# Layer 0 of a four-layer image network: the normalised attention output is loaded and projected by quarters of tokens, its weights by columns, and the bulk loads are placed step by step

## The chip, the cores and the metric

One core of one Trainium2 chip runs the whole program. The metric is the device time of one execution in microseconds (us), here the median of three executions. All arithmetic is fp32. One execution of the program was also recorded by the hardware profiler, and every reading of the profile below is of that execution.

## The reference, cut to what matters

The input `x` is 4 images of 512 channels by 32 x 32 = 1024 positions ("tokens"). Four layers follow one another, each normalising its input by groups of channels and adding its result to the input. Only layer 0 is changed here. It is an attention with 8 heads of 64 channels whose scores are mixed between heads, put through a softmax, and then normalised over each head's whole 1024 x 1024 map (mean, variance, `in_gamma`, `in_beta`):

```
attn = einsum('bhdq,bhdT->bhqT', q, k) * scale
attn = einsum('gh,bhqT->bgqT', w_head, attn)
attn = softmax(attn, axis=-1)
attn = (attn - mean) / sqrt(var + EPS) * in_gamma + in_beta
out  = einsum('bhqT,bhdT->bhqd', attn, v)
out  = out.reshape(b, t, c)
out  = out @ w_proj.T + b_proj
```

The `reshape` takes (head, query, channel of the head) straight to (token, channel). Head h therefore becomes tokens 128h to 128h + 127, and a pair of neighbouring heads becomes one quarter of the tokens. Because mean and variance are those of a whole head, the output `out` of an image can be scaled and projected only after its last query has been processed.

## The kernel before

**Stages.** Layer 0 takes the four images one after the other, until about 1270 us of the span. Then come one layer 2 attention per image and a last stage that looks up the 8 best rows of a memory for each token. The change touches the layer 0 stage alone.

**Steps.** `step` (line 1169) is called for steps s = 0 to 38 of each image; 32 of them (`STEPS`) start a block of 32 queries, the rest let the pipeline run empty. In a step of an image:

- `scores` (L449) multiplies q and k of block s on the TensorE (PE) into two PSUM pairs; the ScalarE (ACT) copies them to the tile `ss` (L455), and eight transfers of 128 KB, four issued by SyncE (SP) and four by GpSimd (POOL), regroup them by head into `s2` (L464). I call these eight the relay. Two tiles `ss` and two `s2` exist.
- `mix` (L475) of block s - 2 multiplies `s2` by the head weights; ACT takes the exponential (L482); the VectorE (DVE) transposes it (L488) and collects sums (L503).
- `apply` (L514) of block s - 7 multiplies the transposed exponentials by v.
- every fourth step `take_out` and `scale` bring the finished 128 queries to the tile `o` and SP stores them to the DRAM tensor `o_rows` (L593).

So the relay of block s must have landed for `mix` in step s + 2, and it must have left `ss` for the copy of step s + 2.

**Work of neighbouring images inside the steps.** While image b runs, the output of image b - 1 is finished: `collect` (L597) loads it back as `of`, in 8 pieces of 256 KB, and then `w_proj` as `w_p`, in 4 pieces of 256 KB; the generator `in_threes` issues three such loads a step, from step 7 on. `instance_norm` (L613) works out the factors in steps 3 to 6 and scales `of` on ACT (L639, 8 instructions) in steps 10, 11 and 12. Steps 12 to 27 (`OUT` = 12) each project one sixteenth: `put_quarter` (L687), four matmuls of 256 columns, then `add_to` and statistics on DVE; every second step ACT loads a piece `xr` of x and SP stores a finished piece to `x1`. At the same time `prepare` (L352) loads image b + 1 once by pieces `xs` for its statistics, and from step 28 (`NEXT`) `next_image` (L269) loads it again as `xn` (8 pieces of 256 KB) with `w_q` (4 pieces), again three loads a step. `normalized` scales `xn` on ACT in steps 30 and 31 and just after, and `take_q` projects it from step 32 on. For the last image the next one is image 0 of layer 2, and `put_out` (L695) projects the last output after the steps.

**Order and queues.** Nearly all instructions are pinned to program order. Bulk loads are issued from ACT's queue by `beside` (L258), and `early` (L1231) issues them between ACT's two `ss` copies of a step. `xn` and `of` share one SBUF place, the tag `xn`, taken in turn; `w_v`, `w_p` and `w_q` share the tag `w2`.

Of the kernel before, what the change touches and what calls it, by code (L numbers as in the profile page):

```python
# [16 lines left out]
P = 128  # L17
# [24 lines left out]
def fast_net(ctx: ExitStack, tc: tile.TileContext, a: dict, out: bass.AP, flag: bass.AP):  # L42
# [169 lines left out]
    dram = ctx.enter_context(tc.tile_pool(name="dram", bufs=1, space=bass.MemoryType.DRAM))  # L212
    x1 = [dram.tile([P, KC, T], F32, tag=f"x1_{b}", name=f"x1_{b}") for b in range(B)]
    x2 = [dram.tile([P, KC, T], F32, tag=f"x2_{b}", name=f"x2_{b}") for b in range(B)]
    o_rows = [dram.tile([P, TC, NB], F32, tag=f"o_{b}", name=f"o_{b}") for b in range(B)]
    r_rows = [dram.tile([NS, NS], F32, tag=f"r_{i}", name=f"r_{i}") for i in range(2)]


# [18 lines left out]
    o_full = eT_flat[:, 2 * KC * T:3 * KC * T]  # L237
    wp_full = eT_flat[:, 3 * KC * T:3 * KC * T + KC * C].rearrange("p (k c) -> p k c", k=KC)

    def big(tag, name):  # L240

        return apool.tile([P, KC, T], F32, tag=tag, name=name)
# [19 lines left out]
    def in_threes(loads):

        for i in range(0, len(loads), 3):
            for out, in_ in loads[i:i + 3]:
                beside(out, in_)
            yield

    def next_image(b, key, src):  # L269

        I = img[b]
        xn = I["xn"] = big("xn", f"xn_{key}{b}")
        w = I[key] = eight_k([P, KC, C], f"{key}_{b}", 2)
        return in_threes([
            (xn[:, k, n * NB:(n + 1) * NB], src[:, k, n * NB:(n + 1) * NB])
            for k in range(KC) for n in range(T // NB)
        ] + [(w[:, k], a[key][:, k]) for k in range(KC)])

    def run_out(gen):
        for _ in gen:  # L280
# [5 lines left out]
    def first():  # L286

        I = img[0]
        xn = I["xn"] = big("xn", "xn_0")
        w = I["w_q"] = eight_k([P, KC, C], "w_q0_0", 0)  # L290
        for k in range(KC):
            nc.sync.dma_start(out=xn[:, k, :], in_=x_v[0, :, k, :])
# [229 lines left out]
    def sums(b, j):  # L522
# [18 lines left out]
        pin(nc.vector.reciprocal(ri, ps))  # L541
        yield

        ok = small.tile([P, 2, NS], F32, tag="ok", name=f"ok_{nm}")
# [34 lines left out]
    def scale(b, j):  # L579


        I = img[b]
        rb = I.pop(("rb", j)).rearrange("p gp (q qq x) -> p qq gp x q", q=4, qq=2)
        pv = I["pv"].rearrange("p gp (qq x q) -> p qq gp x q", qq=2, q=4)
        o = apool.tile([P, KC, NH, NS // 2], F32, tag="o2", name=f"o_{b}_{j}")
        o_v = o.rearrange("p kc (gp r) x -> p r gp x kc", r=2)
        for r in range(2):
            h = slice(r * HD, (r + 1) * HD)
            for par in range(2):
                pin(nc.gpsimd.tensor_mul(  # L590
                    o_v[par * HD:(par + 1) * HD, r], pv[h, par], rb[h, par]))
            yield
        pin(nc.sync.dma_start(  # L593
            out=o_rows[b][:, j, :], in_=o.rearrange("p kc g x -> p (kc g x)")))
        yield

    def collect(b, last):  # L597


        I = img[b]  # L600
        if last:
            I["of"] = o_full
            nc.sync.dma_start(out=wp_full, in_=a["w_proj"])
            nc.sync.dma_start(out=I["of"].rearrange("p (j x) -> p j x", j=TC), in_=o_rows[b])
            return
        I["of"] = big("xn", f"of_{b}").rearrange("p k t -> p (k t)")
        of = I["of"].rearrange("p (j x) -> p j x", j=TC)
        yield from in_threes([(of[:, j], o_rows[b][:, j]) for j in range(6)])
        w = I["w_p"] = eight_k([P, KC, C], f"w_p_{b}", 2)
        yield from in_threes([(of[:, j], o_rows[b][:, j]) for j in range(6, TC)] + [  # L610
            (w[:, k], a["w_proj"][:, k]) for k in range(KC)])

    def instance_norm(b):  # L613


        I = img[b]
        red = small.tile([P, 1], F32, tag="red", name=f"red_{b}")
        pin(nc.vector.tensor_reduce(red, I["ssq"], AX.X, ALU.add))
        yield
        by_head = small.tile([P, NH], F32, tag="ssqh", name=f"ssqh_{b}")  # L620
        nc.gpsimd.tensor_scalar(by_head, of_head, red, None, ALU.mult)
        yield
        ps = small_ps(f"in_{b}")[:, 0:NH]
# [11 lines left out]
        nc.gpsimd.tensor_mul(bb, bb, I["vsum"])  # L635
        yield
        o = I["of"].rearrange("p (jk g x) -> p g jk x", g=NH, x=NS // 2)
        for g in range(NH):
            pin(nc.scalar.activation(  # L639
                o[:, g], o[:, g], AF.Identity, bias=bb[:, g:g + 1], scale=al[:, g:g + 1]))  # L640
            if g % 3 == 2:
                yield

    def out_view(b):
        return img[b]["of"].rearrange("p (j k g x) -> p k g j x", j=TC, g=NH, x=NS // 2)

    def image_piece(b, m, n):
        xr = img[b]["xr", m, n] = apool.tile(
# [11 lines left out]
    def piece_done(b, m, n):  # L660

        I = img[b]
        xr = I["xr", m, n]
        if n == 0:
            I["stb"] = small.tile([P, 2, 6], F32, tag="bnst", name=f"st_b{b}_{m}")
        if n == 0 and m == 0:
            I["mv"] = small.tile([P, KC, 2], F32, tag="mv", name=f"mv_b{b}")
        st, mv = I["stb"], I["mv"]
        pin(nc.vector.bn_stats(st[:, n, :], xr))
        if n == 0:  # L670
            return
        pin(nc.vector.bn_aggr(mv[:, m, :], st.rearrange("p i s -> p (i s)")))
        if m == KC - 1:
            mv1 = I["mv1"] = const.tile([P, 2, KC], F32, tag=f"mv1_{b}", name=f"mv1_{b}")
            pin(nc.vector.tensor_copy(mv1[:, 0, :], mv[:, :, 0]))
            pin(nc.vector.tensor_copy(mv1[:, 1, :], mv[:, :, 1]))

    def put_quarter(b, i):


        I = img[b]
        m, n4 = divmod(i, 4)
        Q = NB // 2
        ps = small_ps(f"p_{b}_{i}")[:, 0:Q]
        o = out_view(b)
        for k in range(KC):
            pin(nc.tensor.matmul(  # L687
                ps, I["w_p"][:, k, m * P:(m + 1) * P], o[:, k, 2 * n4:2 * n4 + 2],
                start=(k == 0), stop=(k == KC - 1),
            ))  # L690
        add_to(b, m, I["xr", m, n4 // 2][:, n4 % 2 * Q:(n4 % 2 + 1) * Q], ps)
        if n4 % 2:
            piece_done(b, m, n4 // 2)

    def put_out(b, m, at):  # L695
# [8 lines left out]
                piece_done(b, m, n)  # L704
                piece_out(b, m, n)

        project(wp_full, lambda k, n: o[:, k, 4 * n:4 * n + 4], m, at, add_out)

# [457 lines left out]
    for m in range(KC):  # L1166
        take_k(0, m, m + 1)

    def step(b, s, mid, piece):


# [6 lines left out]
        tiled = 0 <= j < TC  # L1178
        putting = b > 0 and OUT <= s < OUT + 16
        if b > 0 and OUT < s <= OUT + 16 and s % 2 == 0:  # L1180
            piece_out(b - 1, (s - 2 - OUT) // 4, (s - 2 - OUT) // 2 % 2)
        if s == 0:
            take_v(b, 0)
        if s < STEPS:
            scores(b, s, 0)
            early(b, s)
            scores(b, s, 1)
        if summing and at == 1:
            next(I["tail"])
        if putting:  # L1190
# [16 lines left out]
        if tiled and part == 3:  # L1207
            take_out(b, j)
        if b > 0 and OUT <= s + 1 < OUT + 16 and s % 2:
            image_piece(b - 1, (s + 1 - OUT) // 4, (s + 1 - OUT) // 2 % 2)  # L1210
        if not putting:
            mid(b, s)
        if tiled:
# [11 lines left out]

    OUT, NEXT = 12, 28
    state = {"behind": iter(()), "load": iter(())}

    def early(b, s):  # L1231

        if b > 0 and s == TC - 1:
            state["load"] = collect(b - 1, False)
        if s == NEXT:
            state["load"] = (
                next_image(0, "Wq", x1[0]) if b + 1 == B else next_image(b + 1, "w_q", x_v[b + 1]))
        next(state["load"], None)

    def mid(b, s):  # L1240
        before = b - 1
# [4 lines left out]
        if b > 0:  # L1246
            if s == 3:
                state["norm"] = instance_norm(before)
            if 3 <= s < 7 or OUT - 2 <= s <= OUT:
                next(state["norm"], None)  # L1250
            if s == NEXT:
                state["behind"] = chain(state["behind"], gating(before))
        if NEXT - 4 <= s:
# [11 lines left out]
    for b in range(B):  # L1265
        last = b + 1 == B
        nxt = img[0 if last else b + 1]
        keys = ("Wq", "Wk", "Wv") if last else ("w_q", "w_k", "w_v")
        state.update(held=False, ahead=prepare2(0, True) if last else prepare(b + 1))
        for s in range(STEPS):  # L1270
            step(b, s, mid, piece)
# [823 lines left out]
```

## Time and profile before

| | us |
|---|---|
| median of 3 executions | 2700.16 |
| the three | 2700.16, 2693.87, 2703.72 |
| the profiled execution, device time | 2703.81 |
| its span (first to last instruction) | 2702.0 |
| mean granted TensorE clock | 0.979 of full speed |

| engine | busy us | share of the span |
|---|---|---|
| PE (matmul) | 2581.5 | 96% |
| DVE | 1483.1 | 55% |
| POOL | 1236.2 | 46% |
| ACT | 996.4 | 37% |

The 16 DMA engines moved 349.81 MB, 129 GB/s over the span. Read the table with care: the shares are means over stages with different limits, and a matmul that is slow because the PE has just stood idle still counts as busy. What a stage loses shows in its own stretch of time.

### The profile page before, as it was taken

The numbers are of one execution on the slowest core, as the hardware profiler recorded it, in microseconds if no ns is written. First come the engines' busy times: TensorE is split into PE (matmuls) and PEld (weight loads), VectorE is DVE, ScalarE is ACT, GpSimd is POOL, SyncE is SP. The second block draws the span as 40 slices with busy tenths as digits, with TensorE's granted clock in tenths as the row PEclk, the third lists the DMA queues.
The fourth block names the chain that finished last, engine by engine and source line by source line (L and its number), as shares of the span: only waits on it lengthen the run. The fifth ranks groups of instructions, "written<-read, shape, count | busy, mean of one in ns | idle before, by whom it ended". The sixth has DMA issues, their size and how long they took to land.

```text
span 2702.0 us, 47106 instructions
## 1 busy us (share of the span) xinstructions
PE 2581.5 (96%) x18286; PEld 1156.0 (43%) x18286; DVE 1483.1 (55%) x2387; ACT 996.4 (37%) x1148; POOL 1236.2 (46%) x1891
## 2 busy tenths in 40 slices
PE   8998898989989899999999999999999999999995
PEld 3344433545345443545433443343344344444442
DVE  4487326862478507873145125324513437888886
ACT  1565335551465416651145035215403622121211
POOL 2266315662356524654067027205602626666664
PEclk9999999989999999999999999999999999999997
DMA  2477528881587617785310030021002016667665
GB/s 79 126 217 190 139 83 207 226 222 52 142 225 226 165 60 206 216 216 173 126 47 1 31 124 1 16 83 58 1 32 94 1 58 190 216 190 216 184 182 160
DMA packets 159320, 349.81 MB, mean 129 GB/s; under 512 B 32361, under 2 KB 65129, under 8 KB 155378
## 3 DMA queue, kind: packets, MB, share of 16 engines
q1 hardware_dynamic: 88608, 167.17, 20.4%
q0 software_dynamic: 49152, 142.79, 19.3%
q10 hardware_dynamic: 21330, 36.76, 5.0%
q8 instruction: 147, 2.41, 0.4%
q14 instruction: 83, 0.68, 0.1%
HBM read 178.57 MB, written 33.69 MB: 79 GB/s over the span
## 4 chain that ended last, share of the span: by engine, by line
PE 79%; DMA 5%; DVE 2%; ACT 1%; issue 1%; ACTq 0%; POOL 0%; SPq 0%; POOLq 0%
PE at L1101 16%; PE pair L193 9%; PE sc_c L980 9%; PE pv_c L1013 8%; PE pv L514 5%; PE pair L449 5%; PE p L193 4%; PE pair L475 4%; PE pt L408 3%; PE pt L687 3%; PE k L193 3%; PE q L193 3%; PE v L205 3%; DMA s<-ss 3%; PE rs_c L1034 1%
## 5 line engine op out<-in xcount | busy, mean ns | idle before, releaser
L488 DVE STREAM_TRANSPOSE eT<-e 128x1024 f32<-128x1024 f32 x256 | 315.1, 1231 | 280.8 <-ACT e L482 280.1
L464 POOL DMA_DIRECT2D s<-ss x512 | 259.4, 515 | 450.3 <-ACT ss L455 161.4
L1118 POOL DMA_INDIRECT got<-in_mem,ix x256 | 280.6, 1096 | 215.6 <-DVE tmx L1124 92.1
L503 DVE BATCH_NORM_STATS2 st<-e 128x6 f32<-128x256 f32 x1024 | 350.3, 403 | 1.9 <-POOL sqs L567 1.9
L974 ACT ACTIVATE eT<-sc_c 128x1024 f32<-128x1024 f32 x256 | 247.8, 1022 | 277.8 <-PE sc_c L980 216.4
L482 ACT ACTIVATE e<-pair 128x1024 f32<-128x1024 f32 x256 | 250.5, 1023 | 201.0 <-PE pair L475 179.6
L998 POOL TENSOR_TENSOR e<-eT 128x1024 f32<-128x1024 f32 x96 | 231.4, 2411 | 178.6 <-ACT eT L974 151.9
L455 ACT COPY ss<-pair 128x1024 f32<-128x1024 f32 x256 | 249.4, 1019 | 143.2 <-DMA s<-ss 64.9
L449 PE MATMUL pair<-k,q 64*32 64x512 f32 x4096 | 271.4, 618 | 18.7 <-ACT e L482 9.5
L999 DVE TENSOR_TENSOR eT<-eT,e 128x1024 f32<-128x1024 f32 x96 | 126.2, 1314 | 249.6 <-POOL e L998 249.5
L514 PE MATMUL pv<-eT,v 128*64 128x128 f32 x4096 | 256.9, 280 | 0.0
L514 PEld LDWEIGHTS pv<-eT,v 128*64 128x64 f32 x4096 | 226.6, 139 | 70.1 <-issue 68.5
L980 PE MATMUL sc_c<-q,k 64*128 64x512 f32 x1024 | 238.6, 605 | 2.3 <-DVE xr L653 2.3
L994 POOL TENSOR_TENSOR eT<-eT 128x1024 f32<-128x1024 f32 x32 | 80.6, 2518 | 346.8 <-ACT eT L974 333.6
L1013 PE MATMUL pv_c<-eT,v 128*64 128x512 f32 x1024 | 232.2, 596 | 0.0
L475 PE MATMUL pair<-s,wmix 32*32 32x512 f32 x4096 | 171.1, 630 | 37.1 <-DMA s<-ss 29.7
L1142 DVE SCALAR_TENSOR_TENSOR acc<-got,et,acc 128x512 f32<-128x512 f32 x224 | 168.5, 752 | 8.0
L1040 DVE RECIPROCAL ri_c<-ri_c 128x512 f32<-128x512 f32 x32 | 107.1, 3346 | 96.1 <-ACT ri_c L1039 96.1
L980 PEld LDWEIGHTS sc_c<-q,k 64*128 64x128 f32 x1024 | 94.1, 187 | 132.8 <-issue 73.6
L1106 ACT COPY att<-at 128x1024 f32<-128x1024 f32 x64 | 64.8, 1012 | 218.0 <-PE at L1101 217.8
L449 PEld LDWEIGHTS pair<-k,q 64*32 64x32 f32 x4096 | 59.2, 107 | 186.2 <-ACT e L482 75.3
L1013 PEld LDWEIGHTS pv_c<-eT,v 128*64 128x64 f32 x1024 | 70.4, 137 | 152.8 <-issue 152.2
(294 smaller groups left out, 3295.7 us busy)
## 6 DMA issues: line engine op xcount, KB each, us to landing
s<-ss SPq DMA_DIRECT2D x512, 128.0 KB
s<-ss POOLq DMA_DIRECT2D x512, 128.0 KB
rb<-r POOLq DMA_DIRECT2D x64, 128.0 KB
o<-o SPq DMA_DIRECT2D x32, 256.0 KB
xr<-in_x ACTq DMA_DIRECT2D x32, 256.0 KB
x<-xr SPq DMA_DIRECT2D x32, 256.0 KB
xr_c<-x SPq DMA_DIRECT2D x32, 256.0 KB
x<-xr_c SPq DMA_DIRECT2D x32, 256.0 KB
```

The source lines that it names most:

```text
L193: pin(nc.tensor.matmul(ps[:, n, :], w[:, k, m * P:(m + 1) * P], rhs(k, n), start=(k == 0), stop=(k == KC - 1),))
L449: pin(nc.tensor.matmul(sc[m * NS:(m + 1) * NS, r, :], q[r * HD:(r + 1) * HD, m, s * NS:(s + 1) * NS], k_[r * HD:(r + 1) * HD, m, n * NB:(n ...
L464: pin(relays[side].dma_start(out=s2[2 * m + r::NH], in_=ss[m * NS:(m + 1) * NS, r, :]))
L475: pin(nc.tensor.matmul(mixed(s, r // 2)[t * NS:(t + 1) * NS, r % 2, :].rearrange("p (qq k) -> p qq k", qq=2), wmix[r * NS:(r + 1) * NS], s ...
L482: pin(nc.scalar.activation(e[:, half].rearrange("p r qq k -> p (r qq k)"), flat2(mixed(s, half)), AF.Exp))
L488: pin(nc.vector.transpose(eT[:, j % 2].rearrange("p b (qq i r) x -> p i r qq b x", qq=2, i=4)[:, i, 2 * half:2 * half + 2], e[:, half].rea ...
L503: pin(nc.vector.bn_stats(st[:, i, 2 * half + r, qq, :], e[:, half, r, qq, :]))
L514: pin(nc.tensor.matmul(pv[r * HD:(r + 1) * HD, gp, :], I["v"][:, t, g * HD:(g + 1) * HD], eT[:, j % 2, t, :, 4 * g:4 * g + 4], start=(t == ...
L980: pin(nc.tensor.matmul(sc[:, r, :], I["k"][r * HD:(r + 1) * HD, m, t * P:(t + 1) * P], I["q"][r * HD:(r + 1) * HD, m, n * NB:(n + 1) * NB] ...
L1013: pin(nc.tensor.matmul(pv[r * HD:(r + 1) * HD, :], I["v"][:, t, h * HD:(h + 1) * HD], e[:, r, :], start=(t == 0), stop=(t == TC - 1),))
L1101: pin(nc.tensor.matmul(sc[:, n * NB:(n + 1) * NB], xn3[b][:, k, tt * P:(tt + 1) * P], memT[k][:, i0:i0 + NB], start=(k == 0), stop=(k == K ...
L1118: pin(nc.gpsimd.indirect_dma_start(out=got[:, i, :], out_offset=None, in_=a["mem"], in_offset=bass.IndirectOffsetOnAxis(ap=ix[:, i:i + 1], ...
```

## The change

The layout of `o_rows` becomes [partition, head pair, block of queries, 128] instead of [partition, block, 512], and the tile `o` follows it; each store still has 256 KB, now in runs of 512 bytes in DRAM. One tile `xn_all` is allocated once and serves as `xn` and as `of`, so that parts of it can be loaded and used on their own. The projection runs by quarters: units are ordered by token half first, then by output channels, so that steps 12 to 19 need quarters 0 and 1 of `of` and steps 20 to 27 quarters 2 and 3. The scaling moves to quarters as well (two ACT instructions each in steps 10, 11, 18 and 19). Weights `w_p` and `w_q` are loaded by 128 output columns, in runs of 512 bytes, instead of by 128 input rows, in runs of 2 KB. The three-a-step generator is replaced by a plan that names the loads of each step.

| loads of 256 KB, by step | 7 | 8 | 9 | 10 | 11 | 12 | 13 | 14 | 15 | 16 | 17 | 20, 22, 24, 26 | 28 | 29 | 30 | 31 | 32 | 33 |
|---|---|---|---|---|---|---|---|---|---|---|---|---|---|---|---|---|---|---|
| before | 3 | 3 | 3 | 3 | | | | | | | | | 3 | 3 | 3 | 3 | | |
| after | 2 | 1 | 1 | 1 | 1 | 1 | 1 | 1 | 1 | 1 | 1 | 1 each | 2 | 2 | 1 | 1 | 1 | 1 |

(Rows from 7 to 17 hold for images 1 to 3, the others for all four. Weight columns are the loads of steps 10, 11, 12, 14 and 30 to 33.) `put_out` of the last image now also multiplies by quarters: 64 matmuls of 256 columns where there were 32 of 512. Two small tiles change their number of buffers (`ok` 4 to 2, the statistics `st_b` to one tile of four).

```diff
-    o_rows = [dram.tile([P, TC, NB], F32, tag=f"o_{b}", name=f"o_{b}") for b in range(B)]
+    o_rows = [dram.tile([P, KC, TC, P], F32, tag=f"o_{b}", name=f"o_{b}") for b in range(B)]
+    xn_all = apool.tile([P, KC, T], F32, tag="xn", name="xn_all")
...
     def next_image(b, key, src):
-        I = img[b]
-        xn = I["xn"] = big("xn", f"xn_{key}{b}")
-        w = I[key] = eight_k([P, KC, C], f"{key}_{b}", 2)
-        return in_threes([
-            (xn[:, k, n * NB:(n + 1) * NB], src[:, k, n * NB:(n + 1) * NB])
-            for k in range(KC) for n in range(T // NB)
-        ] + [(w[:, k], a[key][:, k]) for k in range(KC)])
+        def half(k, n):
+            def load():
+                I = img[b]
+                I["xn"] = xn_all
+                beside(xn_all[:, k, n * NB:(n + 1) * NB], src[:, k, n * NB:(n + 1) * NB])
+            return load
+        halves = [half(k, n) for k in range(KC) for n in range(T // NB)]
+        plan = {NEXT - 8 + 2 * i: halves[i:i + 1] for i in range(4)}
+        plan |= {NEXT + i: halves[4 + 2 * i:6 + 2 * i] for i in range(2)}
+        plan |= {NEXT + 2 + m: [load_columns(b, key, a[key], m)] for m in range(KC)}
+        return plan
+    def load_columns(b, key, src, m):
+        def load():
+            I = img[b]
+            if m == 0:
+                I[key] = eight_k([P, KC, C], f"{key}_{b}", 2)
+            beside(I[key][:, :, m * P:(m + 1) * P], src[:, :, m * P:(m + 1) * P])
+        return load
...
-        o = apool.tile([P, KC, NH, NS // 2], F32, tag="o2", name=f"o_{b}_{j}")
-        o_v = o.rearrange("p kc (gp r) x -> p r gp x kc", r=2)
+        o = apool.tile([P, KC, KC, 2, NS // 2], F32, tag="o2", name=f"o_{b}_{j}")
+        o_v = o.rearrange("p gp kc r x -> p r gp x kc")
...
-            out=o_rows[b][:, j, :], in_=o.rearrange("p kc g x -> p (kc g x)")))
+            out=o_rows[b][:, :, j, :], in_=o.rearrange("p gp kc r x -> p gp (kc r x)")))
...
+    def collect(b):
+        of = xn_all.rearrange("p n (j x) -> p n j x", j=TC)
+        def part(n, h):
+            def load():
+                img[b]["of"] = xn_all.rearrange("p k t -> p (k t)")
+                js = slice(4 * h, 4 * h + 4)
+                beside(of[:, n, js], o_rows[b][:, n, js])
+            return load
+        def w(m):
+            return load_columns(b, "w_p", a["w_proj"], m)
+        return {
+            OUT - 5: [part(0, 0), part(0, 1)], OUT - 4: [part(1, 0)], OUT - 3: [part(1, 1)],
+            OUT - 2: [w(0)], OUT - 1: [w(1)], OUT: [w(2)], OUT + 1: [part(2, 0)],
+            OUT + 2: [w(3)], OUT + 3: [part(2, 1)], OUT + 4: [part(3, 0)], OUT + 5: [part(3, 1)],
+        }
...
+    def unit(i):
+        return i // 2 % KC, i // (2 * KC)
     def put_quarter(b, i):
-        m, n4 = divmod(i, 4)
+        m, n4 = unit(i)[0], 2 * unit(i)[1] + i % 2
...
-                ps, I["w_p"][:, k, m * P:(m + 1) * P], o[:, k, 2 * n4:2 * n4 + 2],
+                ps, I["w_p"][:, k, m * P:(m + 1) * P], o[:, n4, k],
...
     def early(b, s):
-        if b > 0 and s == TC - 1:
-            state["load"] = collect(b - 1, False)
-        if s == NEXT:
-            state["load"] = (
-                next_image(0, "Wq", x1[0]) if b + 1 == B else next_image(b + 1, "w_q", x_v[b + 1]))
-        next(state["load"], None)
+        for load in state["plan"].get(s, ()):
+            load()
...
-            if 3 <= s < 7 or OUT - 2 <= s <= OUT:
-                next(state["norm"], None)
+            if 3 <= s < 7:
+                next(state["norm"])
+            if s in (OUT - 2, OUT - 1, OUT + 6, OUT + 7):
+                norm_quarter(before, s % 2 + 2 * (s > OUT))
```

More of the change, by code (lines that the diff above doesn't have):

```diff
@@ L260, in beside @@
         pin(nc.scalar.dma_start(out=out, in_=in_))
[L262 to L267, printed above, removed]
-    def next_image(b, key, src):
-        I = img[b]
-        xn = I["xn"] = big("xn", f"xn_{key}{b}")
-        w = I[key] = eight_k([P, KC, C], f"{key}_{b}", 2)
-        return in_threes([
-            (xn[:, k, n * NB:(n + 1) * NB], src[:, k, n * NB:(n + 1) * NB])
-            for k in range(KC) for n in range(T // NB)
-        ] + [(w[:, k], a[key][:, k]) for k in range(KC)])
+    def next_image(b, key, src):
+        def half(k, n):
[16 more added lines that the diff above has]
+        return load
     def run_out(gen):
@@ L288, in first @@
         I = img[0]
-        xn = I["xn"] = big("xn", "xn_0")
+        xn = I["xn"] = xn_all
         w = I["w_q"] = eight_k([P, KC, C], "w_q0_0", 0)
@@ L542, in sums @@
         yield
-        ok = small.tile([P, 2, NS], F32, tag="ok", name=f"ok_{nm}")
+        ok = small.tile([P, 2, NS], F32, tag="ok", bufs=2, name=f"ok_{nm}")
         rows = r_rows[j % 2]
@@ L593, in scale, with collect_last @@
         pin(nc.sync.dma_start(
-            out=o_rows[b][:, j, :], in_=o.rearrange("p kc g x -> p (kc g x)")))
+            out=o_rows[b][:, :, j, :], in_=o.rearrange("p gp kc r x -> p gp (kc r x)")))
         yield
[L597 to L611, printed above, removed]
+    def collect(b):
[13 more added lines that the diff above has]
+        }
+    def collect_last(b):
+        nc.sync.dma_start(out=wp_full, in_=a["w_proj"])
+        img[b]["of"] = o_full
+        nc.sync.dma_start(
+            out=o_full.rearrange("p (n j x) -> p n j x", n=KC, j=TC), in_=o_rows[b])
     def instance_norm(b):
@@ L635, in instance_norm, with norm_quarter @@
         nc.gpsimd.tensor_mul(bb, bb, I["vsum"])
+        I["norm"] = al, bb
         yield
-        o = I["of"].rearrange("p (jk g x) -> p g jk x", g=NH, x=NS // 2)
-        for g in range(NH):
+    def norm_quarter(b, n):
+        al, bb = img[b]["norm"]
+        o = img[b]["of"].rearrange("p (n jk g x) -> p n g jk x", n=KC, g=2, x=NS // 2)
+        for r in range(2):
+            g = 2 * n + r
             pin(nc.scalar.activation(
-                o[:, g], o[:, g], AF.Identity, bias=bb[:, g:g + 1], scale=al[:, g:g + 1]))
-            if g % 3 == 2:
-                yield
+                o[:, n, r], o[:, n, r], AF.Identity, bias=bb[:, g:g + 1], scale=al[:, g:g + 1]))
     def out_view(b):
-        return img[b]["of"].rearrange("p (j k g x) -> p k g j x", j=TC, g=NH, x=NS // 2)
+        return img[b]["of"].rearrange("p (n j k g x) -> p n k g j x", n=KC, k=KC, g=2, x=NS // 2)
     def image_piece(b, m, n):
@@ L663, in piece_done @@
         xr = I["xr", m, n]
-        if n == 0:
-            I["stb"] = small.tile([P, 2, 6], F32, tag="bnst", name=f"st_b{b}_{m}")
         if n == 0 and m == 0:
+            I["stb"] = small.tile([P, KC, 2, 6], F32, tag="bnst4", bufs=1, name=f"st_b{b}")
             I["mv"] = small.tile([P, KC, 2], F32, tag="mv", name=f"mv_b{b}")
-        st, mv = I["stb"], I["mv"]
+        st, mv = I["stb"][:, m], I["mv"]
         pin(nc.vector.bn_stats(st[:, n, :], xr))
@@ L705, in add_out @@
                 piece_out(b, m, n)
-        project(wp_full, lambda k, n: o[:, k, 4 * n:4 * n + 4], m, at, add_out)
+        ps = place(at, f"proj_{m}")
+        Q = NB // 2
+        for n4 in range(KC):
+            for k in range(KC):
+                pin(nc.tensor.matmul(
+                    ps[:, n4 // 2, n4 % 2 * Q:(n4 % 2 + 1) * Q],
+                    wp_full[:, k, m * P:(m + 1) * P], o[:, n4, k],
+                    start=(k == 0), stop=(k == KC - 1),
+                ))
+        add_out(flat2(ps))
     turn = const.tile([P, 3, P], F32, tag="turn", name="turn")
@@ L1167, in fast_net @@
         take_k(0, m, m + 1)
+    OUT, NEXT = 12, 28
     def step(b, s, mid, piece):
@@ L1180, in step @@
         if b > 0 and OUT < s <= OUT + 16 and s % 2 == 0:
-            piece_out(b - 1, (s - 2 - OUT) // 4, (s - 2 - OUT) // 2 % 2)
+            piece_out(b - 1, *unit(s - 2 - OUT))
         if s == 0:
@@ L1187, in step @@
             scores(b, s, 1)
+        else:
+            early(b, s)
         if summing and at == 1:
@@ L1209, in step @@
         if b > 0 and OUT <= s + 1 < OUT + 16 and s % 2:
-            image_piece(b - 1, (s + 1 - OUT) // 4, (s + 1 - OUT) // 2 % 2)
+            image_piece(b - 1, *unit(s + 1 - OUT))
         if not putting:
@@ L1224, in step @@
             next(I["scale"])
-    OUT, NEXT = 12, 28
-    state = {"behind": iter(()), "load": iter(())}
+    state = {"behind": iter(())}
     def early(b, s):
-        if b > 0 and s == TC - 1:
-            state["load"] = collect(b - 1, False)
-        if s == NEXT:
-            state["load"] = (
-                next_image(0, "Wq", x1[0]) if b + 1 == B else next_image(b + 1, "w_q", x_v[b + 1]))
-        next(state["load"], None)
+        for load in state["plan"].get(s, ()):
+            load()
     def mid(b, s):
@@ L1268, in fast_net @@
         keys = ("Wq", "Wk", "Wv") if last else ("w_q", "w_k", "w_v")
+        state["plan"] = (
+            next_image(0, "Wq", x1[0]) if last else next_image(b + 1, "w_q", x_v[b + 1]))
+        if b > 0:
+            state["plan"] |= collect(b - 1)
         state.update(held=False, ahead=prepare2(0, True) if last else prepare(b + 1))
@@ L1284, in fast_net @@
         if last:
-            run_out(collect(b, True))
+            collect_last(b)
         for m in range(KC):
@@ L1289, in fast_net @@
             run_out(instance_norm(b))
+            for n in range(KC):
+                norm_quarter(b, n)
             bv2 = apool.tile([P, C], F32, tag="o2", name="bv2")
```

## The prediction

> **What bounds the kernel now.** I began with the page: engine shares, then the chain that ended last.
>
> ```profile
> PE 2581.5 (96%) x18286; PEld 1156.0 (43%) x18286; DVE 1483.1 (55%) x2387; ACT 996.4 (37%) x1148; POOL 1236.2 (46%) x1891
> ...
> PE 79%; DMA 5%; DVE 2%; ACT 1%; issue 1%; ACTq 0%; POOL 0%; SPq 0%; POOLq 0%
> ```
>
> The PE carries the end; 5% of 2702 us, 135 us, of the chain are transfers. The chain in order of time shows where. For image 1 (steps 8 to 11, then 28 to 31; columns: start, us, what):
>
> ```profile
> 427.20 5.40 DMA of<-o
> 432.62 12.88 DMA w_p<-in_w_proj
> 445.52 0.54 SPq L464
> 446.05 0.04 issue
> 446.10 7.25 DMA s<-ss
> ...
> 571.85 7.70 DMA xn_w_q<-in_x
> 579.57 12.25 DMA xn_w_q<-in_x
> ```
>
> These are the loads that the change moves. How they hold the PE is seen in ACT's timeline of the same two places (in brackets: idle before, and what ended it):
>
> ```profile
> 441.29 1.01 ACT L455 COPY ss<-pair 128x1024 f32<-128x1024 f32 x1 [5.08 <-DMA s<-ss]
> ...
> 588.55 1.01 ACT L455 COPY ss<-pair 128x1024 f32<-128x1024 f32 x1 [5.75 <-DMA s<-ss]
> ```
>
> The copy of scores waits for the relay of two steps before, which shares the DMA engines with the loads. Next I took engine sums over stretches that I cut at the first exponential (L482) of a step, as the timeline gives it. "Head" is from step 7 to step 13 (images 0 to 3), "tail" from 28 to 33 (images 0 to 3), then a stretch with no bulk loads: steps 12 to 24 of image 0, 12 to 27 of image 1. Columns: stretch, length, then busy us of PE, PEld, DVE, ACT, POOL, then granted clock, DMA share, GB/s.
>
> ```profile
> 128.20:165.90 37.70, 36.11 (x626) 16.57 (x632) 30.99 (x64) 23.49 (x25) 24.56 (x55) 1.00 0.68 191
> 419.50:469.90 50.40, 43.59 (x627) 18.88 (x626) 32.78 (x68) 29.20 (x34) 24.58 (x55) 0.90 0.86 217
> 734.40:783.20 48.80, 40.59 (x627) 18.63 (x626) 32.69 (x68) 29.20 (x34) 24.65 (x55) 0.93 0.88 223
> 1046.20:1089.10 42.90, 40.26 (x627) 18.60 (x626) 31.34 (x65) 28.95 (x33) 24.68 (x55) 0.96 0.94 242
> 262.80:306.10 43.30, 34.09 (x435) 15.48 (x420) 25.73 (x54) 21.58 (x23) 20.52 (x48) 0.88 0.87 220
> 574.60:618.90 44.30, 35.05 (x440) 17.05 (x441) 26.21 (x57) 21.34 (x23) 23.94 (x61) 0.85 0.84 214
> 887.80:930.70 42.90, 33.65 (x440) 16.91 (x440) 26.19 (x57) 21.65 (x23) 24.03 (x61) 0.92 0.86 224
> 1192.70:1239.60 46.90, 35.81 (x440) 17.63 (x440) 27.48 (x58) 20.42 (x23) 24.01 (x61) 0.81 0.92 222
> ...
> 160.60:229.40 68.80, 63.75 (x1160) 29.68 (x1144) 63.83 (x133) 47.85 (x51) 49.78 (x109) 1.00 0.84 232
> 463.90:567.80 103.90, 102.92 (x1570) 59.31 (x1569) 90.89 (x190) 60.46 (x65) 66.00 (x149) 1.00 0.80 225
> ```
>
> Image 0 has no output to collect: its head takes 37.7 us, those of images 1 to 3 up to 50.4. All tails carry loads and drop to a clock of 0.81 to 0.92. Without loads a step costs 68.8/12 = 5.73 us, with a projection 103.9/15 = 6.93 us, where the PE is busy 99% of the time.
>
> **What the Trainium skill says.** "DMA: Bandwidth & Descriptors", section "Issuing engines are not separate DMA queues": transfers from ACT, SP and POOL run on the same 16 engines and interleave. The trace agrees: loads on ACT's queue delay relays on the other two. Same page, "Specifications": the full line rate needs pieces of 512 bytes or more; the new pieces are just 512. The nearest stretch here, the memory stage at 2300 to 2400 us, whose SP queue moves mostly 512-byte packets, took 19.0% of 100 us for 5.77 MB, 3.3 us per MB, against 10.3% of 103.9 us for 3.41 MB, 3.1 us per MB, of ACT's queue in image 1's projection steps. "TensorE: Matmul & The Clock Gate", section "Why this matters for your kernels": gaps over about 3 us bring the slow clock back. In the tails the clock column shows it, so a removed gap also removes slow matmuls behind it; the stretches contain both.
>
> **The change part by part.** Prices: a 256 KB load of 2 KB rows takes 3.1 x 0.262 = 0.82 us of all 16 engines, a column load 0.86.
>
> *Heads.* Without bulk loads an image 1 to 3 head would take image 0's 37.7 plus the one `put_quarter` of step 12, 1.92 us in the chain: 39.6. Four scalings of about 0.75 us on ACT lie in its idle time (23.49 busy of 37.7). That frees 50.4 + 48.8 + 42.9 - 3 x 39.6 = 23.3 us. The new plan still puts two loads in step 7, one in each other; two loads ahead of one relay are 1.6 us, 4.9 over three images if nothing absorbs it, 0 if the relay's spare time does. I take 4.9: head -18.4.
>
> *Tails.* Four free steps are 22.9 us. The scaling of the next image's `xn` (four of 1.24 us, group L380) lengthens steps 30 and 31 by some 1 us on ACT. The last step holds the first q projection: 7.06 + 1.97 + 1.07 of PE = 10.1. Together 34.0 against 43.3, 44.3, 42.9, 46.9 (177.4): 41.4 us. Steps 28 and 29 keep two loads each; with a DMA share of 0.84 x 5.73 = 4.8 us plus 1.64 they need 6.4 us of a 5.73 us step, 0.7 too much: 4 images x 2 x 0.7 = 5.8 given back. The bounds are 0 and the whole 13.1. Tail -35.6. The weight columns of steps 30 to 33 are each used two steps later, so I cost them at nothing; if that cover fails, one waits 0.9 us.
>
> *Projection steps.* They gain up to ten loads per image (images 1 to 3; image 0 gains four). The DMA share goes from 0.80 to 0.80 + 0.85/6.93 = 0.92 in such a step, so all fits on average. Packet records give the cover: in image 1 the last packet of a relay ends 7.0 to 7.4 us after the second `ss` copy, and the copy that needs it starts 11.6 to 12.0 us after: 4.6 us to spare. If nothing absorbed them: 3 x (4 x 0.82 + 2 x 0.86 + 4 x 0.82) + 4 x 0.82 = 28 us. I take 3. Scalings in steps 18 and 19 (1.5 us on ACT) precede the exponentials; ACT waits 2.0 to 2.5 us for `mix` there, so nothing.
>
> *put_out.* 16 groups of four 256-column matmuls at the 1.92 us of group L687 in the chain are 30.7 us against 27.5 for its 32 wide ones: +3.2 on the path (0 if half the columns cost half the time).
>
> *Nothing each:* issuing a DMA of 512 rows takes SP 0.52 us (L1130) against 0.33 to 0.35 for 128 rows, 0.2 us more on an idle queue; it delays the SP half of a relay behind an `o` store by as much. The instruction order of PE, POOL and DVE is otherwise the same but for the order of units; `ok` and `st_b` are used once per four steps and once per image.
>
> Sum: -18.4 - 35.6 + 3 + 3.2 = -47.8 us on the execution's 2703.81, which is 3.65 above the median of the runs: 2700.16 - 47.8 = 2652, rounded to 2653. What is late next in heads and tails is DVE and PE together (63.83 and 63.75 of 68.8).
>
> **Rivals.**
>
> *The loads are only moved* (15%): every load in the projection steps is paid in full, 28 in place of 3: 2653 + 25 = 2678. For it: the same bytes, at a share already 0.80. Against: the `ss` copies of image 1's projection steps wait for the PE, 9.2 of their 9.3 us idle.
>
> *More goes* (14%): heads and tails recover all (-23.3 - 41.4), the projection steps cost nothing, and image 0's stall at 235 to 257 us, which has another cause (below), falls away too: -11.2 + 3.2. 2700 - 72.7 = 2627.
>
> *Tails do not recover* (6%): they would be held by ACT's scalings and POOL's small operations, not by loads: only -18.4 + 3 + 3.2 = -12: 2688. Against: the chain's two `xn` lines, 20 us.
>
> *Slower* (5%): POOL's queue. In image 0, with no load in flight, this occurs:
>
> ```profile
> 232.19 0.20 POOL L151 TENSOR_TENSOR dm_a<-mv_a,gm_a 128x4 f32<-128x4 f32 x1 [4.32 <-DVE gm_a L131]
> ...
> 234.78 2.05 POOL L464 DMA_DIRECT2D s<-ss  x4
> ```
>
> POOL waits for a small DVE result while half a relay stands behind it; the relay lands late, `mix` is late, the next small result is late. Steps 26 and 27 took 8.9 + 13.8 us where two free steps take 11.5: 11.2 us. Loads at steps 13 to 17 and 20 to 26 could eat the 4.6 us of spare time and set this off where it now passes. It decides from (47.8 + 13.5)/11.2, six events, on; twice in each of images 1 to 3 and once more in image 0 are seven: 2653 + 78 = 2731. Against: one load is 0.8 us.
>
> **How the numbers follow.** Forecast 60%: 2653. It is its own 2636 to 2672: the taken-back terms at 0 (4.9 + 5.8 + 3 + 3.2) or at about twice. The range 2632 to 2680 adds the first rival and part of the second and leaves out the fourth, the fifth and half of "more". About 0.5%, 13.5 us, is what a measurement can tell from no change. Faster by more: 60 + 15 + 14 and a third of 6: 91%. Same 4%, slower 5%.
>
> **What would show it.** In the changed profile, the chain's lines `of<-o`, `w_p` and `xn` should be gone or short; heads should be near 41 us, tails near 35.5, both at a clock near 1.00; steps 12 to 27 should keep 6.9 us with a DMA share near 0.9; the last projection should take 30.7 us. I am wrong if ACT's `ss` copies wait for the relay in steps 13 to 27, or if the tails keep 43 us without load lines in the chain.

## The result, and the profile after

| | before | after |
|---|---|---|
| median, us (four executions each, taken side by side) | 2697.11 | 2664.91 |
| lowest to highest, us | 2693.87 to 2703.72 | 2661.94 to 2671.45 |
| ratio of the times, 95% interval | | 0.988 [0.986, 0.9899] |
| span of the profiled execution, us | 2702.0 | 2660.1 |
| mean granted TensorE clock in it | 0.979 | 0.988 |

The change takes 32 us off, 1.2%. The forecast was 47.8 us off. The time lies inside the range, but about a third of the gain is missing.

Some of that third is only a matter of which executions were profiled: the spans differ by 41.9 us, the medians by 32.2. The profiled execution of before (2703.81) lies 6.7 us over the median of 2697.11, and that of after (2661.94) is the fastest of its four. The forecast was a sum of stretches of a profile, so I compare it with the profiles: 41.9 against 47.8. Even there the near agreement is in part luck: one term missed by 18.5 us, and four small surpluses made up 12.6 of them.

The page of after, first the engines, then the chain that ended last:

```profile
PE 2562.5 (96%) x18350; PEld 1165.3 (44%) x18350; DVE 1480.5 (56%) x2387; ACT 996.1 (37%) x1148; POOL 1236.7 (46%) x1891
...
PE 84%; DMA 5%; issue 2%; ACT 2%; DVE 1%; POOL 1%; SPq 0%; ACTq 0%; POOLq 0%
```

The PE's share of the chain rose from 79% to 84%, but transfers still carry 5%. The loads are not all gone from it (start, us, what; the tail of image 1, the head of image 2, the tail of image 3):

```profile
560.02 8.93 DMA xn_all<-in_x
...
730.76 7.55 DMA w_p<-in_w_proj
...
1154.95 7.76 DMA xn_all<-x
```

Beside these it has loads of `w_q` or `Wq` of 1.9 to 5.8 us in the tails of images 0, 1 and 3. What the chain had before the change in images 1 to 3 was longer: `of` and `w_p` 34.3 us in two heads, `xn` 27.8 us in two tails.

What became of the stretches is seen in the next lines. The first three are the heads of images 1 to 3 (steps 7 to 13), the next four the tails of images 0 to 3 (28 to 33), then come the projection steps of images 1 to 3 (13 to 28). Columns as before: length, busy us of PE, PEld, DVE, ACT, POOL, then granted clock, DMA share, GB/s.

```profile
413.00:452.00 39.00, 37.60 (x627) 18.23 (x626) 32.93 (x69) 26.35 (x29) 24.62 (x55) 1.00 0.97 242
713.90:753.90 40.00, 37.88 (x627) 18.15 (x626) 32.95 (x69) 26.46 (x29) 24.79 (x55) 1.00 0.97 238
1013.80:1054.70 40.90, 38.77 (x627) 19.61 (x626) 31.82 (x66) 26.38 (x29) 24.62 (x55) 0.96 0.87 222
261.90:299.50 37.60, 32.19 (x435) 14.88 (x420) 25.66 (x53) 21.33 (x22) 19.82 (x46) 0.95 0.85 224
557.00:598.40 41.40, 34.87 (x441) 17.19 (x441) 26.23 (x57) 21.51 (x23) 24.01 (x61) 0.88 0.80 204
858.80:898.30 39.50, 33.83 (x440) 17.11 (x440) 26.19 (x57) 21.45 (x22) 24.01 (x61) 0.91 0.83 217
1158.50:1200.30 41.80, 33.36 (x440) 17.13 (x441) 26.76 (x56) 20.35 (x22) 24.00 (x61) 0.92 0.90 224
452.00:557.00 105.00, 103.79 (x1574) 60.05 (x1573) 90.94 (x192) 63.05 (x68) 66.18 (x146) 1.00 0.89 245
753.90:858.80 104.90, 103.75 (x1574) 60.12 (x1573) 90.99 (x192) 62.95 (x69) 66.08 (x146) 1.00 0.90 243
1054.70:1158.50 103.80, 103.64 (x1574) 60.09 (x1573) 87.29 (x183) 62.85 (x69) 66.04 (x146) 1.00 0.84 231
```

The same projection steps in before:

```profile
469.90:574.60 104.70, 103.72 (x1574) 60.02 (x1572) 91.58 (x194) 60.38 (x64) 65.97 (x146) 1.00 0.79 221
783.20:887.80 104.60, 103.67 (x1574) 60.04 (x1572) 91.60 (x194) 60.54 (x65) 65.95 (x146) 1.00 0.79 221
1089.10:1192.70 103.60, 103.60 (x1574) 60.10 (x1573) 87.79 (x185) 59.90 (x64) 65.84 (x146) 1.00 0.74 209
```

The heads are mended: 39 to 41 us, two of them at a full clock. The projection steps took the loads in: the DMA share rose from 0.74 to 0.79 before to 0.84 to 0.90, the PE is busy 99% of the time, and the three together are 0.8 us longer. The tails are not mended: three of four need about 40 us or more and still run at a clock of 0.88 to 0.92.

| profiled executions, us | before | after | moved | forecast |
|---|---|---|---|---|
| heads, images 1 to 3 | 142.1 | 119.9 | -22.2 | -18.4 |
| tails, images 0 to 3 | 177.4 | 160.3 | -17.1 | -35.6 |
| projection steps, images 1 to 3 (image 0's 13 to 28: -0.7) | 312.9 | 313.7 | +0.8 | +3, image 0 included |
| last projection (`put_out`) | 27.48 | 27.64 | +0.2 | +3.2 |

What remains of the 41.9 us (some 2.9 us) lies behind the last tail and was not followed.

Within the tails, the missing time is in one place. I write 30→31 for the stretch from the first exponential of step 30 to that of step 31. It took 12.2, 12.2 and 12.9 us in images 1 to 3 before, and takes 12.2, 13.0 and 12.6 us after. Image 0's took 6.5 and takes 6.6, with the same loads in its steps. The stretches in front of it, 28→29 and 29→30, did shrink: from 18.5 to 15.5 us in image 1.

What holds 30→31 is in the timeline of after, image 1 (start, duration, engine and line; in brackets the idle time before it and what ended it):

```profile
569.34 1.01 ACT L464 COPY ss<-pair 128x1024 f32<-128x1024 f32 x1 [5.04 <-DMA s<-ss]
...
570.25 1.02 ACT L464 COPY ss<-pair 128x1024 f32<-128x1024 f32 x1
...
572.58 1.94 ACT L491 ACTIVATE e<-pair 128x1024 f32<-128x1024 f32 x2 [1.32 <-issue]
...
574.81 0.12 DVE L162 TENSOR_SCALAR gve_b<-pt 128x4 f32<-128x4 f32 x1
...
575.01 1.04 POOL L120 TENSOR_TENSOR grstd_b<-gve_b,mhalf 128x4 f32<-128x4 f32 x1 [8.17 <-DVE gve_b L162]
...
577.12 2.08 POOL L473 DMA_DIRECT2D s<-ss  x4 [0.47 <-ACT ss L464]
579.22 0.30 POOL L544 TENSOR_TENSOR sums<-st 128x32 f32<-128x32 f32 x1
...
579.58 0.41 PE L547 MATMUL pt<-sums,same 128*128 128x32 f32 x2 [3.05 <-POOL sums L544]
...
579.91 3.52 PE L523 MATMUL pv<-eT,v 128*64 128x128 f32 x32
...
583.37 1.16 PE L484 MATMUL pair<-s,wmix 32*32 32x512 f32 x32
...
584.78 1.02 ACT L491 ACTIVATE e<-pair 128x1024 f32<-128x1024 f32 x1 [6.80 <-issue]
```

The two copies of block 30's scores end at 571.27. POOL's half of their relay goes out only at 577.12, 5.9 us later, because an instruction in front of it on POOL, a 128x4 power `grstd_b`, has waited 8.17 us for `gve_b`. Behind the relay stands `sums`, late as well at 579.22, and that is what the PE waits for, 3.05 us here and 4.82 us in images 2 and 3. The late relay itself costs step 31 nothing: the mix of step 31 (583.37) takes the scores of block 29, and block 30's are needed a step later. The matmuls behind the wait are slow as well: the 32 of L523 at 579.91 take 3.52 us, where they take 1.97 in the same step of the pinned kernel below. The exponential of step 31 starts at 584.78, 12.2 us after that of step 30. The bracket of the relay names ACT's copy and only 0.47 us. That is the wait that ended last at the relay's own place in the queue. The 5.9 us do not appear there at all; they stand in the line of the small instruction ahead of it.

The Trainium skill's "Perfetto Trace Analysis", section "Tensor Engine Instruction (MATMUL, LD_WEIGHTS)", says in passing that ACT, DVE and GpSimd are strict FIFO. This trace agrees: the copies that the relay needs were done 3.7 us before POOL began `grstd_b`, and it still stayed behind it.

`grstd_b` is one of four small POOL operations of `group_coeffs_parts`, which are pinned to program order only where they have one column (`hold = pin if n == 1`). Those with four columns were free, and the scheduler placed this one ahead of the relay and of `sums`. It belongs to the image before, so image 0 has none, and image 0's 30→31 is short. The change moved nothing here: POOL's order is the same in both kernels. So is the wait: before the change, in image 1,

```profile
595.56 1.04 POOL L120 TENSOR_TENSOR grstd_b<-gve_b,mhalf 128x4 f32<-128x4 f32 x1 [10.37 <-DVE gve_b L162]
...
597.67 2.08 POOL L464 DMA_DIRECT2D s<-ss  x4 [0.47 <-ACT ss L455]
```

### The profile page after: what moved, and what is told of

It is laid out like the page before. It is cut to its first block, busy times and chain, and to the rows that moved or that the text cites. A ratio compares the mean times of both kernels' runs of the same rounds, so it can differ in the third digit from the quotient of the medians.

```text
span 2660.1 us, 47218 instructions
## 1 busy us (share of the span) xinstructions
PE 2562.5 (96%) x18350; PEld 1165.3 (44%) x18350; DVE 1480.5 (56%) x2387; ACT 996.1 (37%) x1148; POOL 1236.7 (46%) x1891
## 4 chain that ended last, share of the span: by engine, by line
PE 84%; DMA 5%; issue 2%; ACT 2%; DVE 1%; POOL 1%; SPq 0%; ACTq 0%; POOLq 0%
PE at L1137 16%; PE sc_c L1016 9%; PE pv_c L1049 8%; PE pair L193 8%; PE pv L523 7%; PE pair L458 5%; PE pair L484 4%; PE p L193 4%; PE pt L417 3%; PE v L205 3%; PE q L193 3%; PE k L193 3%; DMA s<-ss 3%; PE pt L714 3%; ACT e L491 2%
## 5 line engine op out<-in xcount | busy, mean ns | idle before, releaser
L523 PEld LDWEIGHTS pv<-eT,v 128*64 128x64 f32 x4096 | 228.8, 140 | 69.7 <-issue 68.2
L523 PE MATMUL pv<-eT,v 128*64 128x128 f32 x4096 | 259.2, 281 | 0.0
L484 PE MATMUL pair<-s,wmix 32*32 32x512 f32 x4096 | 159.3, 609 | 14.9 <-DMA s<-ss 11.9
```

The source lines that it names most:

```text
L484: pin(nc.tensor.matmul(mixed(s, r // 2)[t * NS:(t + 1) * NS, r % 2, :].rearrange("p (qq k) -> p qq k", qq=2), wmix[r * NS:(r + 1) * NS], s ...
L523: pin(nc.tensor.matmul(pv[r * HD:(r + 1) * HD, gp, :], I["v"][:, t, g * HD:(g + 1) * HD], eT[:, j % 2, t, :, 4 * g:4 * g + 4], start=(t == ...
```

## The experiments

The question was what holds 30→31. The first theory (A in the expectations) is POOL's queue: a free small operation ahead of the relay and of what stands behind it. Its rivals were the loads that the plan still issues in steps 28 to 33, and ACT's scalings of `xn`. In the expectations, "step 31" of a tail is the stretch that ends with step 31's exponential, and steps "26 and 27" of image 0 are the stretch 25→27. Ratios are to runs of the kernel before on the same chip; their medians were 2698.69 for the first four experiments and 2698.35 for the last three. The runs of after were taken at another time, beside runs of before with a median of 2697.11.

**The small operations pinned, in the kernel after (`e1_after_pinned`).** The four small operations keep their place in the program; nothing else changes. (Behind layer 0, where the list `by_scalar` is no longer empty, they stay free.)

```diff
-        hold = pin if n == 1 else lambda ins: ins
+        hold = (lambda ins: ins) if by_scalar else pin
```

> The changed kernel with the small POOL operations of group_coeffs_parts kept in program order, so that the reciprocal root of image b's statistics (L120) stands behind the relays of steps 30 and 31 and not ahead of them. Theory A (what the tails still lose is POOL's queue: half a relay stands behind a small operation that waits for DVE): step 31 of images 1 to 3 falls from 12.2 to 13.0 us to 6 to 7 us, image 0's steps 26 and 27 from 22.7 us together to about 12; total 18 + 10 us less than the changed kernel, about 2637 us, ratio to before near 0.978. Theory B (the two loads left in steps 28 and 29 and the weight columns hold the relay; POOL's wait follows from that): tails keep their 38 to 42 us, at most 5 us less, 2660 us.

Measured: 2635.57 us (2633.87 to 2639.36), ratio 0.9769 [0.9746, 0.9792], 29 us under after. The tails of images 1 to 3 (stretches as above):

```profile
548.50:581.80 33.30, 30.91 (x440) 15.30 (x440) 26.07 (x57) 21.32 (x22) 24.34 (x57) 1.00 0.92 251
843.20:877.60 34.40, 30.70 (x440) 15.24 (x441) 26.10 (x57) 21.28 (x23) 24.48 (x57) 1.00 0.93 240
1136.20:1172.80 36.60, 30.64 (x441) 15.23 (x441) 26.30 (x55) 20.35 (x21) 23.97 (x60) 1.00 0.92 249
```

They lost 18.4 us together, and 30→31 fell to 6.9, 6.5 and 6.5 us. The number of matmuls is the same (440), but they count 30.6 to 30.9 us busy in place of 33.4 to 34.9, at a clock of 1.00 in place of 0.88 to 0.92. That agrees with what the prediction cited of "TensorE: Matmul & The Clock Gate", if not as a sharp edge. In after the PE stands idle for 2.98 and 3.05 us in the tail of image 1 and for 4.82 us in those of images 2 and 3. Pinned, no gap in images 1 and 2 is over 1.6 us, and image 3 keeps its clock through one of 3.10 us. The same place in the timeline, image 1:

```profile
558.09 1.01 ACT L464 COPY ss<-pair 128x1024 f32<-128x1024 f32 x1 [2.34 <-DMA s<-ss]
...
559.00 1.02 ACT L464 COPY ss<-pair 128x1024 f32<-128x1024 f32 x1
...
560.99 2.06 POOL L473 DMA_DIRECT2D s<-ss  x4 [1.15 <-PE pt L156]
...
562.69 0.12 DVE L162 TENSOR_SCALAR gve_b<-pt 128x4 f32<-128x4 f32 x1
...
563.07 0.30 POOL L544 TENSOR_TENSOR sums<-st 128x32 f32<-128x32 f32 x1
...
563.43 0.41 PE L547 MATMUL pt<-sums,same 128*128 128x32 f32 x2 [0.79 <-POOL sums L544]
...
567.85 2.03 POOL L473 DMA_DIRECT2D s<-ss  x4 [2.69 <-PE pair L484]
...
569.94 1.04 POOL L120 TENSOR_TENSOR grstd_b<-gve_b,mhalf 128x4 f32<-128x4 f32 x1
```

Block 30's relay leaves 1.0 us after its copies and `sums` follows at once, so the PE waits 0.79 us for it and no longer 3.05. Block 31's relay is next, and only then comes `grstd_b`, which finds `gve_b` 7 us old. Over the whole program, the view of the tile `grstd_b` says what ended POOL's idle time before its instructions. After has, in us and times,

```profile
its engine sat idle before it (us, times) until:
  DVE gve_b L162: 18.7, 3
  DVE gate L918: 2.8, 2
```

and with the small operations pinned the first of these lines is gone:

```profile
its engine sat idle before it (us, times) until:
  DVE gate L918: 2.9, 2
```

The other part of the gain is in image 0. The stall that the prediction had described there fell from 22.7 us (25→27, in before and after alike) to 12.0. The two parts, 18.4 + 10.7 = 29.1 us, are close to the 29.3 us between the medians, and more than the 26.3 us between the profiled spans (2660.1 and 2633.8): some other stretches are a little longer here.

**The same edit in the kernel before (`e2_before_pinned`).** This shows whether the change and the stall depend on one another.

> The kernel before, with the same small POOL operations kept in program order and nothing else. Theory A: image 0's steps 26 and 27 lose their stall (about 10 us), and the tails of images 1 to 3 lose what POOL adds (up to 6 us each) but keep what the twelve loads cost; 10 to 28 us less than before, 2670 to 2687 us. Theory B: no change in tails, at most the 10 us of image 0. If pinning alone brought as much as the whole change (32 us), the loads would have been a trigger of the POOL stall and little else.

Measured: 2672.86 us, ratio 0.9896 [0.9867, 0.9925]. Image 0's 25→27 fell from 22.7 to 11.9 us, and 30→31 of images 1 to 3 to 6.8, 7.6 and 6.9. The stretch that the threes of loads hold remained: 29→30 takes 10.7, 9.6 and 10.2 us here, against 6.7, 8.0 and 9.4 with the change. The edit is worth 26 us here and 29 in after. The change is worth 32 us without it and 37 with it (2672.86 - 2635.57). The two losses lie in different steps and nearly add.

**Only the heads changed (`e3_tail_threes`).** The next image's loads go back to three a step from step 28, on top of after:

```diff
-        plan = {NEXT - 8 + 2 * i: halves[i:i + 1] for i in range(4)}
-        plan |= {NEXT + i: halves[4 + 2 * i:6 + 2 * i] for i in range(2)}
-        plan |= {NEXT + 2 + m: [load_columns(b, key, a[key], m)] for m in range(KC)}
-        return plan
+        loads = halves + [load_columns(b, key, a[key], m) for m in range(KC)]
+        return {NEXT + i: loads[3 * i:3 * i + 3] for i in range(4)}
```

> The changed kernel with the loads of the next image (eight halves, four weight columns) put back to three a step in steps 28 to 31; heads as changed. Both theories: heads stay at 39 to 41 us; tails go back to the 43 to 47 us of before, 17 us in sum, 2682 us, ratio near 0.994. If tails stay near 40 us, the spread of these loads was worth nothing and something else in the change shortened them.

Measured: 2681.24 us, ratio 0.994 [0.9919, 0.9961]. Tails 44.2, 44.2, 43.8 and 48.4 us, as long as before or longer; heads 38.7, 40.0 and 39.2 us in images 1 to 3, as short as after.

**Only the tails changed (`e4_head_threes`).** The output's loads go back to three a step from step 7:

```diff
-        return {
-            OUT - 5: [part(0, 0), part(0, 1)], OUT - 4: [part(1, 0)], OUT - 3: [part(1, 1)],
-            OUT - 2: [w(0)], OUT - 1: [w(1)], OUT: [w(2)], OUT + 1: [part(2, 0)],
-            OUT + 2: [w(3)], OUT + 3: [part(2, 1)], OUT + 4: [part(3, 0)], OUT + 5: [part(3, 1)],
-        }
+        loads = [part(n, h) for n in range(KC) for h in range(2)] + [w(m) for m in range(KC)]
+        return {OUT - 5 + i: loads[3 * i:3 * i + 3] for i in range(4)}
```

> The changed kernel with the loads of the output (eight pieces, then four weight columns) put back to three a step in steps 7 to 10; tails as changed. Both theories: tails stay at 38 to 42 us, heads go back to 43 to 50 us, 22 us in sum, 2687 us, ratio near 0.996. If the heads stay near 40 us, it is the scaling by quarters or the order of units that shortened them and not the spread of loads.

Measured: 2679.11 us, ratio 0.9925 [0.9903, 0.9948], 8 us better than I expected. The profiled execution, 2683.42, is the slowest of its four and lies nearer to what I expected. Heads 49.9, 50.7 and 42.7 us in images 1 to 3, as before; tails 34.5, 39.9, 39.6 and 45.1. The quarters, the layout of `o_rows` and the weight columns are in both of these kernels, and each keeps the old time where it has the old plan: by themselves they bring nothing that shows. Each of the two gains comes with its plan: against the 2698.69 of before, the kernel with the heads alone gains 17 us and that with the tails alone 20. Here, with the small operations free, 30→31 stays at 12.2 us in images 1 to 3.

**Loads of the tail one step later (`e5_pinned_later`).** With the small operations pinned, the tails (142.2 us in sum) are still 6 us over the 4 x 34.0 of the prediction's reference. The prediction blamed the two loads each in steps 28 and 29 for 5.8 us. This variant of `e1_after_pinned` spreads them:

```diff
-        plan |= {NEXT + i: halves[4 + 2 * i:6 + 2 * i] for i in range(2)}
-        plan |= {NEXT + 2 + m: [load_columns(b, key, a[key], m)] for m in range(KC)}
+        c = [load_columns(b, key, a[key], m) for m in range(KC)]
+        plan |= {NEXT: halves[4:5], NEXT + 1: halves[5:7], NEXT + 2: halves[7:8],
+                 NEXT + 3: c[0:1], NEXT + 4: c[1:2], NEXT + 5: c[2:4]}
```

> The kernel of e1 (small POOL operations in program order) with the loads of steps 28 to 33 moved back: one half in step 28, two in 29, one in 30, one weight column each in 31 and 32, two in 33 (e1: two, two, then one column each in 30 to 33). Theory A (what e1's tails still have over 34 us is the pair of loads in steps 28 and 29, which makes the relay of step 28 late for step 30): step 30 falls from 6.7 to 10.2 us to about 6 us, tails to about 34 us each, 4 to 8 us less than e1, about 2630 us. Rival: the weight columns, now one step later, are waited for by the q projection in steps 34 and 35, or step 30 keeps its length because ACT's scaling of xn sets it; then the time is e1's, 2636 us, or up to 4 us more.

Measured: 2635.4 us (2632.15 to 2646.21), ratio 0.9778 [0.9754, 0.9802]. Tails 35.7, 33.8, 37.5 and 35.7 us, 142.7 in sum. Nothing gained: 29→30 and 30→31 traded a microsecond or two, and the kernel without this edit, run beside it on the same chip, took 2631.3 (next experiment), 4 us less. That a pair of loads in one step costs 0.7 us is neither shown nor refuted. What the last 6 us are made of stays open. The chain of `e1_after_pinned` still has loads of `xn` at the tails of images 1 to 3, 6.8, 6.0 and 3.4 us.

**The best version again (`e1_again_5_rounds`).** The kernel of `e1_after_pinned`, on the chip of `e5_pinned_later`, which is another than that of its first run.

> The kernel of e1 again, beside the one above on the same chip, because the difference looked for is a few us: 2634 to 2640 us.

Measured: 2631.3 us (2628.82 to 2637.99), ratio 0.9757 [0.9737, 0.9778]. It beats both kernels: 2.4% under before and 1.3% under the median of after.

**How much more the projection steps would hide (`e6_two_more`).** After, with two more 256 KB copies (DRAM to DRAM, of a part of `x` to a place that nothing reads) on ACT's queue behind each bulk load of steps 12 to 27: 20 in each of images 1 to 3 and 8 in image 0, 68 in all. The small operations are free, as in after. The edit stands inside the loop over the loads of a step:

```diff
+            if OUT <= s < NEXT:
+                for i in range(2):
+                    beside(junk[turn_j[0] % 8], x_v[b, :, i, 0:NB])
+                    turn_j[0] += 1
```

> The changed kernel with two more copies of 256 KB, DRAM to DRAM and used by nobody, issued from ACT behind each bulk load in steps 12 to 27: 20 in each of images 1 to 3, 8 in image 0, 68 in all. It measures how much room those steps have left. If the relay's spare time of about 4.6 us absorbs them as it absorbed the loads: at most 8 us more, 2665 to 2673 us, steps 12 to 27 at most 107 us per image. If there is no room left, each is paid in full at 0.82 us of the DMA engines: 56 us more, 2721 us. If they set off the POOL stall as in image 0, single steps of images 1 to 3 grow by 5 us and more.

Measured: 2688.07 us, ratio 0.9962 [0.9951, 0.9972], 23 us over after. That lies between the first two expectations, about 40% of the price in full, which is an estimate from loads and was not measured for copies within DRAM. The steps 13 to 28 grew by 4.3, 9.3, 11.6 and 5.9 us in images 0 to 3, 31 us together; the profiled spans differ by 26. Image 1 and image 2:

```profile
453.40:567.70 114.30, 107.27 (x1574) 60.46 (x1573) 91.56 (x195) 63.55 (x69) 66.04 (x146) 1.00 0.95 271
763.50:879.90 116.40, 109.68 (x1574) 60.92 (x1573) 91.45 (x194) 63.16 (x69) 65.86 (x146) 1.00 0.95 263
```

The growth is not even. In image 1, 13→14 takes 10.9 us (6.8 in after), 14→15 8.9 (7.1) and 17→18 11.3 (7.6), and the steps from 20 on don't grow; in image 2, 21→22 and 22→23 grow as well. No step grows by the 5 us that the third expectation took for a stall on POOL. What ACT's copies waited for in image 1's steps 13 to 28 (engine, line, releaser; us in total, times, longest), first with the copies added,

```profile
ACT ss L466 <- DMA s<-ss: 14.9, 4, 6.1
...
ACT ss L466 <- PE pair L460: 7.2, 9, 1.1
```

and in after:

```profile
ACT ss L464 <- PE pair L458: 8.4, 11, 1.0
...
ACT ss L464 <- DMA s<-ss: 6.5, 3, 2.4
```

With one load a step ACT's copies wait mostly for the PE, which is the bound. With two more they wait most for the relay: 14.9 us in four waits where there were 6.5 in three. The room in the projection steps is real and it has an end, which this change does not reach.

## Why the prediction was right in its time and wrong in its tails

**Right: the bound and the heads.** Of the chain's lines in the heads, those of `of` are gone and one of `w_p` is left, 7.55 us in image 2, and the heads fell to 39.0, 40.0 and 40.9 us where about 41 was said. The 4.9 us that I took back for the two loads in step 7 was nearly nothing (22.2 us gained of the full 23.3); the lower of the two bounds held. Putting the threes back restored 49.9, 50.7 and 42.7 us, so the loads were the cause.

**Right: the loads moved into the projection steps are hidden.** +0.8 us in images 1 to 3 and -0.7 in image 0, for +3 forecast. The rival "the loads are only moved" priced them at 28 us. That the room is limited is shown by the copies of `e6_two_more`.

**Wrong: the tails.** The step that failed is "Four free steps are 22.9 us ... Together 34.0": it takes for granted that the steps of a tail run free once the loads are out of the way. They recovered 17.1 us of 35.6, and in image 2 the sign that the prediction had named came nearly as it said: a tail of 39.5 us without a load in the chain. The missing 18.5 us are not the loads': pinned, with every load where it was, the tails of images 1 to 3 fell by a further 18.4 us, and the sum of all four, 142.2, is what I had forecast for the change alone (177.4 - 35.6 = 141.8). The prediction had both halves of this in hand and didn't join them. It described POOL's wait for image 0 and used it only for the rival "slower" and for a stall that might fall away under "more goes". It did not ask where else in the image a free small operation stands ahead of a relay. And it had the last link only in part: it said that the relay lands late and so `mix` is late. In before the PE does wait for the relay there, 2.09 us at 240.94, but it waits longer, 5.07 us, for `sums` behind it:

```profile
251.96 0.64 PE L538 MATMUL pt<-sums,same 128*128 128x32 f32 x2 [5.07 <-POOL sums L535]
```

The rival "tails do not recover" names POOL's small operations, but I set the chain's two `xn` lines, 20 us, against it. Those lines were right about 28→30 (they end at 591.82, just before step 30's exponential at 593.1) and silent about 30→31, another 12.2 us. Of that rival, the small operations were the half that is shown; that ACT's scalings hold little follows from the pinned tails, which contain all of them and are 6 us over the reference in sum.

**Wrong in size: the last projection.** +0.2 us instead of +3.2. The price of 1.92 us for four 256-column matmuls came from groups that stand alone between other work. When 16 such groups follow one another, it is 1.73 us (27.64 / 16). The two chains, before and after (start, us, what; the trace counts two records for a matmul):

```profile
1328.99 27.48 PE pair L193 x64
...
1288.04 27.64 PE pair L738 x128
```

The lower bound of 0 was the right one. (The forecast's sum, 2652.4, rounds to 2652 and not to 2653; that changes nothing.)

**The rivals.** "Slower" did not happen: image 0's stretch with POOL's wait is 22.7 us in both kernels, and no projection step of images 1 to 3 grew by more than 1 us. "More goes" (2627) failed in after, but the pinned version comes within 4 to 9 us of its time, by the way it named, the stall in image 0 falling away, together with the tails.

## What to carry to other kernels

Read an instruction that is late by the queue it stands in: its own bracket shows only the last wait, and the cause is in the idle time of an instruction ahead of it, here a 128x4 power with 8.17 us before it and half a relay behind it. Then ask what the bound engine waits for: here it was not the late relay but a 128x32 sum behind it. When a wait is found to be late in one place, look for the same instruction pattern at every other place before a removed load is credited with the whole stretch. When most instructions are pinned, the few that are left free are worth a look: these four cost 26 us in one kernel and 29 in the other.

## What the runs showed of the hardware

- 64 matmuls of 256 columns took as long as 32 of 512 when they follow one another, 27.64 against 27.48 us, so in a stream the half width cost nothing.
- Runs of 512 bytes were not free, though no queue's total shows it. In after, the weight columns on ACT's queue (7.34 MB in 14336 packets of 512 bytes) took 4.4 us of the 16 engines per MB by the packet records, the loads left in runs of 2 KB (29.38 MB, `of` among them) 3.4. So the prediction's citation, that pieces of 512 bytes suffice for the full line rate, does not hold on this queue as far as packet times under load tell. The queue's share still stays 5.0%, since its 2 KB packets took 3.6 us per MB before, when the loads stood closer together:

```profile
q10 hardware_dynamic: 21330, 36.76, 5.0%
...
q10 hardware_dynamic: 32082, 36.76, 5.0%
```

- Issuing one 256 KB load held ACT's queue for 0.55 us in runs of 512 bytes and for 0.33 us in runs of 2 KB (medians of `w_p` and of `xn_all` from `o` in after).
- A DMA share of 0.84 to 0.97 over a stretch of 39 to 105 us, with one load a step and two in step 7, left the heads of after at 39.0 to 40.9 us, where 39.6 was the estimate without loads, and the projection steps 0.8 us longer in three images. At 0.95, with two copies within DRAM beside each load, the projection steps of images 1 and 2 grew by 9.3 and 11.6 us. So the share alone doesn't tell. That the bytes ahead of one relay decide fits what ACT's copies waited for, and was not tested apart.
